# Three edits to the order of work in a four-layer graph kernel: an earlier tile load, fewer tests ahead, logarithms kept together

## The chip, the cores and the metric

The kernel runs on one core of a Trainium2 chip. The time is that of the device, in microseconds (us), for one whole execution. The kernel before has a median of 806.51 us over 3 runs (806.50 to 806.54).

The core has a matmul engine (PE, with its weight loads shown apart as PEld), a vector engine (DVE), a scalar engine that evaluates functions from tables (ACT), a general engine (POOL) and a queue processor (SP). Each runs its own instructions in order. DMA transfers run beside them and are started by SP, ACT or POOL.

## What is computed

`x` is 4096 x 64 and `adj` is a 4096 x 4096 matrix of zeros and ones, about one in 128 a one. Four layers follow each other, each of the form x = x + layer(relu(layernorm(x)), adj):

```python
# layer 0: the entries of a row of adj are weighted by their rank
rank = cumsum(adj != 0, axis=1); deg = rank[:, -1:]
k = minimum(deg, 100);  pos = rank - (deg - k)
w = mask * where(pos > 0, 0.5 ** (k - pos), 0)
out = w @ (h @ weight) + bias
# layer 1: attention over all pairs, then masked by adj
att = adj * sigmoid((2 + 2 * qm @ k.T) / att_scale + att_bias)
support = att @ h1;  out = support / norm(support)
# layer 2: two gated steps
m = adj @ (x @ W); r, z = sigmoid(...); n = tanh(i_n + r * h_n)
x = (1 - z) * n + z * x
# layer 3: hyperbolic aggregation; tanh and artanh of row norms
XW = mobius_matvec(W, X); num = adj @ (gamma * XW); den = adj @ (gamma - 1)
out = expmap0(relu(logmap0(midpoint(num, den, alpha))))
```

Each layer is thus dominated by a product with `adj`. In layer 1 a 4096 x 4096 matrix of sigmoids is also made and masked. In layer 3 artanh is worked out with logarithms.

## The kernel before

**Tiles.** `adj` is used transposed. It is cut into four quarters `q` of 1024 columns and 32 blocks `b` of 128 rows: 128 tiles of 128 x 1024, taken in the order `tiles[n]`, quarter after quarter, with `b` falling from 31 to 0. All tiles stay on the chip as 8-bit floats in `A8` ("A" in the profile). Most come through POOL's queue, whose DMA casts them on the way. The tiles with `direct(n)`, that is n = 0, 1 and every n with n % 8 = 4, come as 32-bit floats through SP's queue into a buffer "whole", and are cast on an engine (`cast0`: tiles 0 and 1 half on ACT and half on DVE, the others on DVE).

**Tests.** The fast path holds only if `adj` is made of zeros and ones. So `checks()` (lines 1102 to 1130) tests every tile in its 32-bit form on DVE, one instruction of 1.22 us each. Tiles that came directly are tested in the buffer that they came in; the other 110 are loaded again through SP, as "whole", for the test alone. The list `depth[0]` says how many such loads may be ahead of the test: 1 at first, 2 from the middle of layer 0's first quarter, still 2 in layer 1, and 4 from layer 2 on. Loads issue as soon as the pool gives a buffer. A last small matmul (flag_ps) collects the result.

**A shared pool.** `b4p` has six buffers of 128 x 1024 floats. They serve the "whole" tiles and the sigmoid tiles "sig" of layer 1 in turn. A new tile waits until the last reader of the buffer's old content is done.

**The planner.** The kernel is built by a Python program that writes every engine's order. `Weave` keeps an estimated time for each engine. The main loops (layer 0's and layer 1's sums, and so on) issue their matmuls directly. Side work is written as generators that yield single operations (`Op`), kept in two lists: `work` for what later stages need, and `back` for the tests. `begin(op)` (line 677) estimates when an operation could start; `fill` issues side operations that fit ahead of the main loop's next one on DVE or ACT with a margin `late`, and `draw` issues what fits beside the matmuls. So a small change of an estimate or of a margin may move many instructions, but only in order.

**Layer 0** (to about 234 us). `stream0` makes running counts with matmuls (cnt, with the constant matrices tri and upd), turns them on ACT or DVE into weights w, and sums w times h (acc, with h in two parts hm and lo). Before that, x is loaded by quarters (`load_x`) and normalized in `pre0`; quarter 3 is needed first. The first loads go through SP in the order tile 0, x of quarter 3, tile 1, x of quarter 2, tile 2 (lines 878 to 883).

**Layer 1** (about 234 to 500 us). For each quarter and each pair of blocks, `stream1` makes the scores on PE (16 matmuls for two half quarters), ACT writes their sigmoid into a "sig" buffer, DVE multiplies it by A, and 16 matmuls add it to acc. The first of two pairs of blocks is weighed at once, the second between older sums (`later`). At the end of each quarter `post1` reads acc out (mt, agg), turns it (ps_n), and prepares layer 2's input (ps_t turns the next one).

**Layer 2** (about 500 to 650 us) runs two steps; each sums A times hm and lo, and works out gates r, z and n (rz and ih on PE, from mx tiles loaded through SP). **Layer 3** (to about 790 us) sums A times S. `pre3` prepares S for each quarter: it forms the norms of h and of the product mxn, calls `lengths` (a maximum and an inverse root on DVE), then `artanh2` (two logarithms on ACT) and a tanh. `post3` does the like for the output. `preload(func)` is a one-element ACT operation that brings in a function's table early; sigmoid and tanh share a table, the logarithm has another.

**Lines in the profile.** All instructions that go through the class `Engine` are recorded with L781; PE's matmuls and transposes have L973 and L977. Which work a row belongs to is told by the tile names.

Of the kernel before, what the change touches and what calls it, by code (L numbers as in the profile page):

```python
# [12 lines left out]
AF = mybir.ActivationFunctionType  # L13
# [580 lines left out]
class Op:  # L594


    def __init__(self, e, dur, ins, outs, run, kinds=()):
        self.e, self.dur, self.ins, self.outs, self.run, self.kinds = e, dur, ins, outs, run, kinds


def names(*aps):
# [3 lines left out]
class Weave:  # L605
# [10 lines left out]
    def __init__(self):  # L616
        self.t = dict.fromkeys("PDAGS", 0.0)
        self.at, self.used = {}, {}
        self.banks = {1: [0.0] * 8}
        self.kind = {}  # L620
        self.work, self.back, self.width = [], [], 2
        self.late = 0.0
        self.quiet = False
        self.dma = 0.0
        self.busy = False
        self.table = None
        self.tiled = 0

    def ready(self, e, ins, outs=(), kinds=()):
        s = 0.0  # L630
# [46 lines left out]
            (self.work if piece in self.work else self.back).remove(piece)  # L677

    def begin(self, op):
        return max(self.t[op.e], self.ready(op.e, op.ins, op.outs, op.kinds))  # L680

    def issue(self, piece):
# [62 lines left out]
TABLES = {AF.Sigmoid: 0, AF.Tanh: 0, AF.Ln: 1, AF.Exp: 2}  # L745


class Engine:
# [12 lines left out]
    def __getattr__(self, name):  # L761
        fn, w = getattr(self.real, name), self.weave

        def call(*args, **kw):
            outs = names(args[0], kw.get("accum_out"))
            ins = names(*args[1:], *(v for k, v in kw.items() if k != "accum_out"))
            n = max(math.prod(a.shape[1:]) for a in args if isinstance(a, bass.AP))
            dur = self.cost(name, n) if name != "dma_start" else 0.1
            if "accum_out" in kw:
                dur += 0.08  # L770

            def run():
                more = 0.0
                if name == "activation" and args[2] in TABLES:
                    more = 1.3 if w.table != TABLES[args[2]] else 0.0
                    w.table = TABLES[args[2]]
                w.book(self.e, dur + more, ins, outs)
                if name == "dma_start":
                    for k in outs:
                        w.land(k, 1.4 if "whole" in k else 0.8)  # L780
                return fn(*args, **kw)  # L781

            if self.later:
                return Op(self.e, dur, ins, outs, run)
            if self.e in "DA":
                w.fill(self.e, w.ready(self.e, ins, outs) + w.late)
            return run()
        return call
# [3 lines left out]
def fast_kernel(ctx: ExitStack, tc: tile.TileContext, t: dict, out: bass.AP, flag: bass.AP):  # L792
# [24 lines left out]
    weave = Weave()  # L817
# [56 lines left out]
    def load_x(q, eng):  # L874
        xq[q] = b2(f"x{q}")
        eng.dma_start(xq[q], x_nm[:, q * QB:(q + 1) * QB, :])

    weave.dma = 0.5
    load0(0)
    load_x(3, Y_)  # L880
    load0(1)
    load_x(2, Y_)
    load0(2)

# [215 lines left out]
    depth = [1]  # L1100
# [246 lines left out]
    def stream1():  # L1347

        acc, behind = [], []

        def add(c, q, i, gs):
            if i == 0:
                acc.append(one(f"acc{c}"))
            for j in range(2):
                b = 2 * i + j
                mm(acc[c][j * D:(j + 1) * D, :], S1[b // QB][:, b % QB, :], gs[c][:, j, :],
                   start=i == 0, stop=i == NB // 2 - 1)

        def add_behind(more=()):
            q, i, gs = behind.pop(0)  # L1360
            for c in (0, 1):
                add(c, q, i, gs)
                if more:
                    more.pop(0)()
                weave.draw(weave.quiet)
            if i == NB // 2 - 1:
                weave.finish()
                weave.add(post1(q, acc[:]))
                acc.clear()

        def turn(q, i, later=None):
            if q == 0 and i % (QB // 2) == 0:
                weave.until((1, i // (QB // 2)), DONE)
            weave.quiet = (1, NQ - 1) not in DONE
            weave.late = 2.0 if weave.quiet else 1.0
            gs = ahead[:] if (q, i) == (0, 0) else []
            for c in range(len(gs), 2):
                ps = score(q, i, c)
                if later is None:
                    gs.append(weigh(q, i, c, ps))  # L1380
                else:
                    later.append(lambda q=q, i=i, c=c, ps=ps: gs.append(weigh(q, i, c, ps)))
                weave.draw(weave.quiet or c == 1)
            behind.append((q, i, gs))
            if i == 8:
                load1(q + 1)

        for q in range(NQ):
            for i in range(0, NB // 2, 2):

                later = []
                turn(q, i)
                turn(q, i + 1, later)
                while len(behind) > 2:
                    add_behind(later)
                for go in later:
                    go()
                if len(behind) > 1:
                    add_behind()
        add_behind()  # L1400
# [193 lines left out]
        yield from pre3(q)  # L1594


    def lengths(s):

        yield DV.tensor_scalar(s, s, NORM_EPS2, None, op0=ALU.max)
        r = yield from rsqrt(s)  # L1600
        n = stat("norm", s.shape[1])
        yield DV.tensor_tensor(n, s, r, ALU.mult)
        return n, r
# [5 lines left out]
    def preload(func):  # L1609

        yield AC.activation(void, tab, func)

    def artanh2(x, between=()):

        nb = x.shape[1]
        xc = stat("axc", nb)
        yield DV.tensor_scalar(xc, x, ARTANH_BOUND, None, op0=ALU.min)
        q, r = stat("at", nb), stat("ln", nb)
        yield AC.activation(q, xc, AF.Ln, bias=ones)
        yield AC.activation(r, xc, AF.Ln, bias=ones, scale=-1.0)  # L1620
        yield from preload(AF.Tanh)
        low = small.tile([P, ST], I32, tag="st", name="flow")[:, :nb]
        yield DV.tensor_scalar(low, xc, 0.25, None, op0=ALU.is_lt)
        x2, p = stat("x2", nb), stat("po", nb)
        yield DV.tensor_tensor(x2, xc, xc, ALU.mult)
        yield DV.tensor_scalar(p, x2, *(2.0 * c for c in ARTANH_POLY[:2]), op0=ALU.mult, op1=ALU.add)
        yield DV.tensor_tensor(p, p, x2, ALU.mult)
        for c in ARTANH_POLY[2:-1]:
            yield DV.scalar_tensor_tensor(p, p, 2.0 * c, x2, op0=ALU.add, op1=ALU.mult)
        yield DV.tensor_tensor(q, q, r, ALU.subtract)  # L1630
        yield DV.scalar_tensor_tensor(p, p, 2.0 * ARTANH_POLY[-1], xc, op0=ALU.add, op1=ALU.mult)
        yield from between
        yield DV.copy_predicated(q, low, p)
        return q
# [3 lines left out]
    def pre3(q):  # L1638
# [9 lines left out]
        for i, v in enumerate((hn, mx)):  # L1648
            sq = b2("sq")
            yield AC.activation(sq, v, AF.Square)  # L1650
            yield DV.tensor_reduce(ss[:, i * QB:(i + 1) * QB], sq, AX.X, ALU.add)
        yield from preload(AF.Ln)
        n, r = yield from lengths(ss)
        mr, c = r[:, QB:], stat("ratio", QB)
        yield DV.tensor_tensor(c, n[:, QB:], r[:, :QB], ALU.mult)
        a = yield from artanh2(n[:, :QB])
# [144 lines left out]
    def post3(parts3, sgn, den, ss):  # L1801

        nb = CB * len(parts3)
        part = [slice(i * CB, (i + 1) * CB) for i in range(len(parts3))]
        vs = [n65[:, :, :D] for u, (n65, al) in parts3]
        yield from head3(len(parts3) - 1, parts3[-1][1], sgn, den, ss)  # L1810
        yield from preload(AF.Ln)
        rd = yield from recip(den)
        n, r = yield from lengths(ss)
        t = stat("t", nb)
        yield DV.tensor_tensor(t, n[:, :nb], rd, ALU.mult)
        ratio = stat("ratio", nb)

        def between():
            yield DV.tensor_tensor(ratio, n[:, nb:], r[:, :nb], ALU.mult)

        a = yield from artanh2(t, between())
        for h, (u, (n65, al)) in zip(part, parts3):
            yield DV.scalar_tensor_tensor(a[:, h], a[:, h], 0.25, al, op0=ALU.mult, op1=ALU.mult)
        yield DV.scalar_tensor_tensor(a, a, ARTANH_MAX, ratio, op0=ALU.min, op1=ALU.mult)
        yield AC.activation(a, a, AF.Tanh)
        yield DV.tensor_tensor(a, a, r[:, nb:], ALU.mult)
        for h, v, (u, (n65, al)) in zip(part, vs, parts3):
            yield DV.scalar_tensor_tensor(v, v, 0.0, rows(a[:, h]), op0=ALU.max, op1=ALU.mult)
            x = X[u // 2][:, (u % 2) * CB:(u % 2 + 1) * CB, :]
            yield DV.tensor_tensor(x, x, v, ALU.add)  # L1830
            yield SY.dma_start(out_nm[:, u * CB:(u + 1) * CB, :], x)
# [8 lines left out]
    weave.add(pre0(NQ - 2))  # L1840
    stream0()
    lead[0] = math.inf
    stream1()
    depth[0] = 4
    for step in range(2):
# [89 lines left out]
```

## Time and profile before

| what | us |
|---|---|
| median of 3 runs | 806.51 |
| the profiled execution, time | 807.01 |
| its span in the trace | 805.1 |
| PE busy | 767.5 |
| DVE busy | 635.6 |
| ACT busy | 432.2 |
| POOL busy | 61.6 |

The profiled execution takes 1.9 us more than its span, and lies 0.5 above the median. The mean granted clock of PE is 0.993. In a row of the profile, "out<-in" names the tile written and the tiles read, x and a number the count of instructions. "[0.81 <-ACT sig]" means that the engine stood idle for 0.81 us before it, and that ACT's work on sig ended that. The groups in which most of the tests and of layer 1 lie are these (busy, mean ns of one | idle before, releaser):

```profile
L781 ACT ACTIVATE sig<-score,fatt_add,fatt_mul 128x512 f32<-128x512 f32 x256 | 179.2, 779 | 57.1 <-DVE whole L781 25.2
L781 DVE TENSOR_TENSOR sig<-sig,A 128x1024 f32<-128x1024 f32 x128 | 154.9, 1223 | 29.9 <-ACT sig L781 25.5
L781 DVE SCALAR_TENSOR_TENSOR whole<-whole 128x1024 f32<-128x1024 f32 x128 | 153.2, 1220 | 4.6 <-DMA whole<-in_adjT 4.0
L973 PE MATMUL score<-qd,kT 64*128 64x512 f32 x512 | 126.3, 612 | 1.5 <-ACT sig L781 1.5
L973 PE MATMUL acc<-sig,S 128*64 128x512 f32 x512 | 120.2, 601 | 4.2 <-DVE sig L781 3.9
```

### The profile page before, as it was taken

To read this page: it belongs to the slowest core of one execution; us is meant where nothing else is said; L and a number is where in the kernel's file an instruction comes from. 1 tells how busy PE (TensorE), PEld (TensorE's weight loads), DVE (VectorE), ACT (ScalarE), POOL (GpSimd) and SP (SyncE) were. 2 spreads that over 40 slices of the span, in tenths; PEclk is the share of its full clock that TensorE was granted. 3 is DMA by queue.
4 is the path that set the end of the run, shared out by engine and by line. 5 is a ranking of instruction groups with operands and counts; after the bars stand their busy time and mean duration, and the time that the engine had idled before them with its cause. 6 is when DMAs were issued, how large, how long until landed. Compare 5 with 4: busy or idle time off the path is not lost.

```text
span 805.1 us, 12309 instructions
## 1 busy us (share of the span) xinstructions
PE 767.5 (95%) x4473; PEld 369.7 (46%) x4494; DVE 635.6 (79%) x1419; ACT 432.2 (54%) x756; POOL 61.6 (8%) x125
## 2 busy tenths in 40 slices
PE   5999999999999999998999999999999999999992
PEld 2334444544443333332333333444444444599992
DVE  6886867777777988988888898978789387685895
ACT  5655555565566777887787785113220245444333
POOL 3333233231000000000000000000000000000000
PEclk9999999999999999999999999999999999999997
DMA  9999999999601033013104006696888300000010
GB/s 220 153 174 193 217 163 207 205 177 207 183 34 40 0 118 93 25 59 99 52 25 130 30 1 210 225 361 215 287 304 313 76 8 20 1 2 2 9 35 17
DMA packets 43956, 98.41 MB, mean 122 GB/s; under 512 B 5104, under 2 KB 20464, under 8 KB 43888
## 3 DMA queue, kind: packets, MB, share of 16 engines
q1 hardware_dynamic: 25888, 78.98, 29.0%
q0 software_dynamic: 15840, 14.42, 19.1%
q10 hardware_dynamic: 2160, 4.14, 1.4%
q8 instruction: 37, 0.61, 0.3%
q14 instruction: 31, 0.25, 0.1%
HBM read 135.54 MB, written 5.24 MB: 175 GB/s over the span
## 4 chain that ended last, share of the span: by engine, by line
PE 80%; DVE 9%; ACT 6%; issue 2%; DMA 1%; SPq 0%; ACTq 0%; DVEq 0%
PE acc L973 50%; PE cnt L973 13%; PE score L973 10%; ACT sig L781 5%; DVE sig L781 3%; DVE whole L781 2%; PE rz L973 2%; PE ps_l L973 2%; DMA whole<-in_adjT 1%; PE ps_t L977 1%; PE ih L973 1%; ACT w L781 1%; DVE ss L781 1%; PE ps_kq L973 1%; DVE w L781 1%
## 5 line engine op out<-in xcount | busy, mean ns | idle before, releaser
L781 ACT ACTIVATE sig<-score,fatt_add,fatt_mul 128x512 f32<-128x512 f32 x256 | 179.2, 779 | 57.1 <-DVE whole L781 25.2
L781 DVE TENSOR_TENSOR sig<-sig,A 128x1024 f32<-128x1024 f32 x128 | 154.9, 1223 | 29.9 <-ACT sig L781 25.5
L781 ACT ACTIVATE w<-cnt 128x512 int16<-128x512 f32 x198 | 111.6, 595 | 88.6 <-PE cnt L973 85.7
L781 DVE SCALAR_TENSOR_TENSOR whole<-whole 128x1024 f32<-128x1024 f32 x128 | 153.2, 1220 | 4.6 <-DMA whole<-in_adjT 4.0
L973 PE MATMUL score<-qd,kT 64*128 64x512 f32 x512 | 126.3, 612 | 1.5 <-ACT sig L781 1.5
L973 PE MATMUL acc<-sig,S 128*64 128x512 f32 x512 | 120.2, 601 | 4.2 <-DVE sig L781 3.9
L973 PE MATMUL acc<-A,hm 128*128 128x512 fp8e4 x512 | 115.4, 379 | 0.0
L973 PEld LDWEIGHTS <-hm 128*128 128x128 bf16 x768 | 73.6, 98 | 90.3 <-issue 8.2
L973 PE MATMUL cnt<-A,ftri 128*128 128x512 fp8e4 x256 | 98.2, 386 | 8.2 <-ACT A L781 8.2
L973 PE MATMUL cnt<-A,fupd 128*128 128x512 fp8e4 x248 | 95.4, 385 | 4.0 <-ACT w L781 1.7
L973 PE MATMUL acc<-S,A 128*128 128x196 bf16 x1024 | 88.0, 246 | 0.0
L973 PEld LDWEIGHTS <-A 128*128 128x128 fp8e4 x1024 | 87.0, 96 | 1.3 <-issue 1.2
L973 PEld LDWEIGHTS score<-qd,kT 64*128 64x128 f32 x512 | 50.5, 186 | 72.0 <-issue 46.7
L973 PE MATMUL acc<-w,hm 128*128 128x512 bf16 x235 | 70.6, 379 | 0.9 <-issue 0.2
L781 DVE TENSOR_SCALAR w<-cnt 128x512 int16<-128x512 f32 x58 | 40.1, 691 | 39.5 <-PE cnt L973 38.3
L973 PEld LDWEIGHTS acc<-sig,S 128*64 128x64 f32 x512 | 32.5, 136 | 83.5 <-issue 40.8
L857 POOL DMA_DIRECT2D A<-in_adjT x110 | 59.9, 546 | 131.5 <-DMA A<-in_adjT 130.7
L973 PEld LDWEIGHTS <-lo 128*64 128x64 bf16 x768 | 39.8, 109 | 50.3 <-issue 21.3
L973 PE MATMUL acc<-A,lo 128*64 128x512 fp8e4 x512 | 58.9, 380 | 0.0
L781 ACT ACTIVATE mt<-acc 64x512 f32<-64x512 f32 x32 | 19.0, 592 | 74.2 <-PE acc L973 64.5
L973 PEld LDWEIGHTS <-ftri 128*128 128x128 bf16 x256 | 24.8, 98 | 47.4 <-issue 20.5
L1676 POOL MEMSET S<- 128x4 bf16 x8 | 0.9, 115 | 537.3 <-DVE xT L781 463.8
(185 smaller groups left out, 634.7 us busy)
## 6 DMA issues: line engine op xcount, KB each, us to landing
whole<-in_adjT SPq DMA_DIRECT2D x128, 512.0 KB, 6.7
A<-in_adjT POOLq DMA_DIRECT2D x110, 128.0 KB, 14.0
qd<-qs SPq DMA_DIRECT2D x16, 128.0 KB, 4.4
mx<-gs SPq DMA_DIRECT2D x16, 128.0 KB, 7.6
xT<-gs SPq DMA_DIRECT2D x8, 256.0 KB, 6.9
x<-in_x SPq DMA_DIRECT2D x6, 256.0 KB, 6.1
xs<-x SPq DMA_DIRECT2D x4, 256.0 KB, 6.0
qs<-qT ACTq DMA_DIRECT2D x4, 256.0 KB, 4.9
```

The costliest lines, as they stand in the source:

```text
L781: return fn(*args, **kw)
L857: nc.gpsimd.dma_start(A8[q][b // 2][:, b % 2, :], a)
L973: nc.tensor.matmul(o, lhsT, rhs, start=start, stop=stop, skip_group_check=True)
L977: nc.tensor.transpose(o, src, ident)
L1676: nc.gpsimd.memset(S3[q, c][:, :, 3 * e:], 1.0)
```

## The change

There are three parts, and no instruction is added or taken away; all of them move work in order.

1. Tile 1 of `adj` is issued on SP's queue ahead of x of quarter 3.
2. Before layer 1 starts, `depth[0]` is set to 1, so only one tile is loaded ahead of its test there; it goes to 4 after layer 1 as before. In the same loop the margin `late` is 0.8 instead of 1.0 once all of layer 1's inputs are made.
3. The preload of the logarithm's table moves from in front of `lengths` to behind its first operation. From there until the second logarithm has been issued, the planner holds back (`held`) every side operation whose function has another table.

```diff
     def begin(self, op):
+        if self.held and op.table not in (None, TABLES[AF.Ln]):
+            return math.inf
         return max(self.t[op.e], self.ready(op.e, op.ins, op.outs, op.kinds))
...
-                return Op(self.e, dur, ins, outs, run)
+                return Op(self.e, dur, ins, outs, run,
+                          table=TABLES.get(args[2]) if name == "activation" else None)
...
     load0(0)
+    load0(1)
     load_x(3, Y_)
-    load0(1)
     load_x(2, Y_)
     load0(2)
...
-            weave.late = 2.0 if weave.quiet else 1.0
+            weave.late = 2.0 if weave.quiet else 0.8
...
-    def lengths(s):
+    def lengths(s, log=False):
 
         yield DV.tensor_scalar(s, s, NORM_EPS2, None, op0=ALU.max)
+        if log:
+            yield from preload(AF.Ln)
+            weave.held += 1
         r = yield from rsqrt(s)
...
         yield AC.activation(r, xc, AF.Ln, bias=ones, scale=-1.0)
+        weave.held -= 1
         yield from preload(AF.Tanh)
...
-        yield from preload(AF.Ln)
-        n, r = yield from lengths(ss)
+        n, r = yield from lengths(ss, True)
...
     lead[0] = math.inf
+    depth[0] = 1
     stream1()
     depth[0] = 4
```

The same replacement of the two lines stands in `pre3` and in `post3`. `Op` takes the new argument `table`, and `Weave` starts with `held` at 0.

More of the change, by code (lines that the diff above doesn't have):

```diff
@@ L594, with __init__ @@
 class Op:
-    def __init__(self, e, dur, ins, outs, run, kinds=()):
+    def __init__(self, e, dur, ins, outs, run, kinds=(), table=None):
         self.e, self.dur, self.ins, self.outs, self.run, self.kinds = e, dur, ins, outs, run, kinds
+        self.table = table
 def names(*aps):
@@ L627, in __init__ @@
         self.tiled = 0
+        self.held = 0
     def ready(self, e, ins, outs=(), kinds=()):
@@ L1810, in post3 @@
         yield from head3(len(parts3) - 1, parts3[-1][1], sgn, den, ss)
-        yield from preload(AF.Ln)
         rd = yield from recip(den)
-        n, r = yield from lengths(ss)
+        n, r = yield from lengths(ss, True)
         t = stat("t", nb)
```

## The prediction

> **What bounds the kernel now.** I read the busy table first, then what the matmul engine (PE) waited for, then PE's stretches by stage, and last the timeline round the waits. The busy table, as engine, busy us, share, instructions:
>
> ```profile
> PE 767.5 (95%) x4473; PEld 369.7 (46%) x4494; DVE 635.6 (79%) x1419; ACT 432.2 (54%) x756; POOL 61.6 (8%) x125
> ```
>
> PE works 767.5 of 805.1 us, so what an edit can bring is what PE loses now: 37.6 us, of which some 14.5 are the tail after PE's last dense work (790.6 to 805.1) and some 21 are single gaps. The waits of PE say who owns them (total us, times, longest):
>
> ```profile
> PE cnt L973 <- ACT A L781: 8.2, 2, 5.9
> PE acc L973 <- DVE sig L781: 3.9, 8, 1.0
> PE ps_n L977 <- ACT sig L781: 2.3, 3, 0.8
> PE ps_o L977 <- DVE xT L781: 1.6, 1, 1.6
> PE score L973 <- ACT sig L781: 1.5, 3, 0.5
> ```
>
> The first row is the start of the kernel, the rows with sig are layer 1, the row with ps_o is layer 3. By stage (length, then busy us of PE, PEld, DVE, ACT, POOL, granted clock, DMA share, GB/s), two quarters of layer 1 and three stretches after it:
>
> ```profile
> 317.11:380.65 63.54, 61.30 (x264) 21.81 (x264) 55.26 (x76) 48.91 (x73) 0.00 (x0) 1.00 0.22 67
> 380.65:444.19 63.54, 61.30 (x264) 21.81 (x264) 55.25 (x76) 48.90 (x73) 0.00 (x0) 1.00 0.22 67
> ...
> 500.00:560.00 60.00, 60.00 (x367) 26.80 (x365) 49.60 (x98) 14.46 (x26) 0.00 (x0) 1.00 0.81 278
> 560.00:650.00 90.00, 90.00 (x543) 38.76 (x543) 67.20 (x118) 17.15 (x30) 0.00 (x0) 1.00 0.69 228
> 650.00:730.00 80.00, 78.37 (x641) 51.72 (x638) 56.88 (x197) 37.72 (x78) 0.81 (x7) 1.00 0.03 8
> ```
>
> Layer 2 leaves PE no gap at all; in layer 1 every quarter repeats the same loss. Inside a quarter the undisturbed cycle is 16 score matmuls (a step of 3.72 us) and 16 acc matmuls (3.58), so 7.30; eight cycles are 58.4, and ps_n and ps_t add about 0.6 each, so about 59.7 against the measured 63.54: near 3.8 us are lost per quarter, all about its boundary. There the timeline (start, us, engine) shows the mechanism:
>
> ```profile
> 378.49 1.23 DVE L781 SCALAR_TENSOR_TENSOR whole<-whole 128x1024 f32<-128x1024 f32 x1
> 379.64 0.08 DVE L781 DVE_READ_ACCUMULATOR whole<-whole 128x1 f32 x1
> 379.64 1.22 DVE L781 TENSOR_TENSOR sig<-sig,A 128x1024 f32<-128x1024 f32 x1
> 379.82 1.45 ACT L781 ACTIVATE sig<-score,fatt_add,fatt_mul 128x512 f32<-128x512 f32 x2 [1.35 <-DVE whole L781]
> 380.65 0.66 PE L977 MATMUL ps_n<-fident,agg 128*128 128x128 f32 x4 [0.81 <-ACT sig L781]
> ```
>
> The sigmoid of ACT writes a buffer of the six-buffer pool that a test (whole) had held. It can't start before the test ends; it stood 1.35 us. PE, which needs ACT to empty the score banks, then stood 0.81. The next score group at 384.82 also takes 4.60 us from start to next start instead of 3.72.
>
> **What the Trainium skill says.** "ScalarE: Activation LUTs", section "What ACT_TABLE_LOAD costs", gives 1283 ns for a table load plus about 1380 ns of drain. This trace agrees with the load (1.28 us) but not with the drain on this path: the load at 708.05 is followed by an ACT instruction at 709.35, 1.30 later. I use 1.28. "TensorE: Matmul & The Clock Gate", Part 1, says that the array runs at half speed until it has been busy for some 3.4 us. The trace agrees in kind: the cnt matmuls step by 0.43 us up to 14.7 us and by 0.215 after. "DMA: Bandwidth & Descriptors", section "Queues, rings and completion order", says that each DMA engine takes the descriptors of a row in ring order. The trace agrees: SP issued tile 0, x, tile 1, and they were usable at 5.23, 5.85 and 9.34.
>
> **The change part by part.**
>
> *Start.* Tile 1 now goes ahead of x (quarter 3). Here is the present wait, and what DVE does meanwhile:
>
> ```profile
> 5.87 0.42 DVE L781 TENSOR_REDUCE mean<-x 128x4 f32<-128x256 f32 x1 [0.19 <-DMA x<-in_x]
> ...
> 9.36 0.63 ACT L781 ACTIVATE A<-whole 128x512 fp8e4<-128x512 f32 x1 [1.72 <-DMA whole<-in_adjT]
> ...
> 10.04 0.58 PE L973 MATMUL cnt<-A,ftri 128*128 128x512 fp8e4 x1 [2.25 <-ACT A L781]
> ```
>
> PE stands 2.25 us for tile 1. The packets of x hold the queue some 1.3 us (x is 256 KB, and tile 1 with 512 KB took the rest of the 3.5 us between landings), so tile 1 should land near 8.0 and PE restart near 8.7: 1.3 gained at most. What pays for it: x lands near 9.3, and its mean, centring and square (0.42+0.42+0.43), which lay in the wait, now come after the cast of tile 1. The normalizing chain on DVE ends about 1.0 later, and the cast of tile 4, now behind hm in DVE's order (14.26 before), starts at about 14.6 and not earlier. Tile 4 is then ready at about 15.3 against 15.00 before. The tiles that POOL's queue brings after it came only 1.1 to 1.3 us ahead of their use, so an earlier PE runs into them. Bounds: 0.3 lost to 1.1 gained. I take 0, because the chain of supply after tile 1 isn't any faster.
>
> *Layer 1.* With two tests ahead, two of the six buffers hold waiting tests and sig turns on four. With one ahead it turns on five. In the order of DVE's instructions after the change, a test stands at least three steps ahead of the sigmoid that takes over its buffer, where it now stands one or two ahead; a step is 1.22 us. So the ACT stalls behind tests (1.35 above, up to 2.3) should go. Per boundary that gives, in PE's own gaps: acc 0.35+0.58, score 0.50, ps_n 0.81, the slow score group 0.88, and 0.17 for each of the four gaps because the ends are modelled (a step is 0.17 longer than the gap alone shows): 3.7 in all. The second and third boundary give 3.7 each. At the first, a test waits for its transfer (DVE idle 1.02 at 292.25), which the change doesn't touch, and about 2.7 goes. The end of layer 1 (two gaps of 0.26, two steps of some 0.17) gives 0.5. Sum 10.6; the bound from below is 0, if the stalls come back one step elsewhere. DVE then works 55.3 less one test of 1.3, so 54.0 of 59.7 us (90%), and ACT 48.9 (82%): tight, but PE stays the slowest. Replaying the orders by hand with these durations left PE about 1.3 us of cover at the tightest sig. I take 10.0. The smaller margin of `late` (0.8 for 1.0) belongs to the same order and isn't priced apart.
>
> *What is moved out of layer 1.* One test fewer per quarter, four or five in all, goes to layer 2: 1.30 us of DVE each beside a PE that is busy anyway (DVE 49.6 of 60 and 67.2 of 90), and one more 512 KB load each in SP's queue, which delivers one per about 1.27 us there. The mx loads of the first gates stand behind one more: 1.3 later against about 1.6 of slack. The second gates' mx loads are issued about five tests later (6 us), but landed some 11 us ahead of use, and their matmuls stand 3 us later in PE's order. Cost 0; without the cover 1.3 to 6.
>
> *Table.* In layer 3 the last gates and the last logarithms share ACT:
>
> ```profile
> 704.29 1.28 ACT L781 ACT_TABLE_LOAD   x1
> ...
> 708.05 1.28 ACT L781 ACT_TABLE_LOAD   x1
> ...
> 709.57 1.28 ACT L781 ACT_TABLE_LOAD   x1
> 710.86 0.69 ACT L781 ACTIVATE z<-rz,gate_b 128x512 f32<-128x512 f32 x1
> ...
> 718.93 0.63 PE L977 MATMUL ps_o<-fident,xT 128*128 128x128 f32 x4 [1.63 <-DVE xT L781]
> ```
>
> The instructions and the number of table loads are the same after the change (64 loads); only their order differs. The squares go first, then the three loads stand in one run, the tanh of the logarithm's chain comes some 3 us earlier, and z and the n gate follow it. The wait of ps_o, 1.63, should be covered, since ps_o also stands four matmul groups later. Bounds: 0 to 1.7 gained; I take 1.6. The tail after 790 keeps ACT's order, and is priced at 0.
>
> *Sum.* −10.0 − 1.6 + 0 = −11.6 on the profiled execution's 807.0, so 795.4. The runs' median (806.51) lies 0.5 below that execution; I keep half of it and say 795.2.
>
> **The rivals.** *Partly (24%).* DVE at 90% is nearly in lockstep with PE, and each boundary still adds two mt and agg steps and one test. If half of the layer-1 loss comes back behind DVE, it is −5.0 − 1.6: 800. For it: the idle time of DVE behind ACT sig is 24.0 us over layer 1, so the two follow one another closely. Against it: that idle time is mostly the same stalls seen from the other side.
>
> *Nothing (4%).* The stalls are only relabelled, since four sig and two tests share six buffers in whatever order. Then only the table's 1.6 and small losses in layer 2 are left: 806.5. Against it: the lead in steps that the new order shows.
>
> *Slower (12%).* With one tile ahead a test finds its data not landed. DVE takes its instructions in order, so every sig behind it stands. The loads need 3.8 to 5.5 us to land in this stage; the new order leaves seven to nine DVE steps (8.5 us and more) between release and test. It decides if that lead shrinks below four steps, as for the test at 292.25, which waited 1.02. At 1.02 for each of some 20 tests, with 0.3 caught by PE's cover, it is +14.4, against −11.6: 809.8.
>
> **How the numbers follow.** The likeliest case, 60%, gives 795.2, with its own range 792.5 to 798. A difference of 0.2% (1.6 us) is about what a measurement of this kernel can tell from no change. The range has to leave out the 12% and the 4% and little else: low end from the full 10.6, the full start gain of 1.1 and 1.7 from the table, 793.4, less 1; high end past the partly case to 804. Faster: 60+24 = 84%; same 4%; slower 12%.
>
> **What would show it.** In the changed profile: "ACT sig <- DVE whole" far below 25.2; quarters of layer 1 near 60 us between ps_n groups; no ps_n, score or acc waits on sig over 0.3 after the first boundary; PE's first wait in tile 1 shorter, but tile 4's matmul still near 15; no wait of ps_o on xT; no PE gap between 500 and 650. A new row "DVE whole <- DMA whole" of several us in layer 1, or a gap at rz or ih in layer 2, would prove me wrong.

## The result and the profile after

The changed kernel takes 797.38 us (median of 4 runs, 797.15 to 798.03) against 806.50 in the same setting: the ratio is 0.9889, 95% interval 0.9872 to 0.9906. It is faster by 9.1 us; 11.3 was forecast. The profiled execution went from 807.01 to 797.43, its span from 805.1 to 795.6.

PE's waits of the changed kernel, as total us, times, longest:

```profile
PE cnt L978 <- ACT A L785: 5.8, 2, 5.4
PE cnt L978 <- DVE A L785: 2.3, 1, 2.3
...
PE acc L978 <- DVE r L785: 1.2, 1, 1.2
PE acc L978 <- DVE sig L785: 1.0, 1, 1.0
```

The waits of ps_n and score on sig are gone, and of eight waits of acc on sig the one at layer 1's very start is left. Two rows are new: one on the cast of tile 4 (DVE A), at the start, and one on DVE r, in layer 3. The two quarters of layer 1 that answer to those shown before (length, then busy us of PE, PEld, DVE, ACT, POOL, clock, DMA share, GB/s) now leave PE no gap, and are 3.4 us shorter each:

```profile
315.77:375.93 60.16, 60.16 (x266) 22.04 (x265) 54.38 (x74) 48.20 (x73) 0.00 (x0) 1.00 0.21 62
375.93:436.08 60.15, 60.15 (x265) 22.04 (x264) 54.38 (x74) 48.14 (x72) 0.00 (x0) 1.00 0.20 62
```

The timeline at the end of the first of them shows why:

```profile
373.77 2.11 ACT L785 ACTIVATE sig<-score,fatt_add,fatt_mul 128x512 f32<-128x512 f32 x3
373.99 1.23 DVE L785 SCALAR_TENSOR_TENSOR whole<-whole 128x1024 f32<-128x1024 f32 x1
...
375.14 2.35 DVE L785 TENSOR_TENSOR sig<-sig,A 128x1024 f32<-128x1024 f32 x2
...
375.93 0.66 PE L982 MATMUL ps_n<-fident,agg 128*128 128x128 f32 x4
```

ACT runs through three sigmoids in a row, past the end of the test, where before it stood 1.35 us for the test's buffer. ps_n starts without a wait. ACT's wait for tests in layer 1 fell from 25.2 us to this (total us, times, longest):

```profile
ACT sig L785 <- DVE whole L785: 1.8, 2, 1.2
```

The same marks in both traces split the difference. The marks are the start of PE's last cnt matmul, the start of the fourth quarter's ps_n, and the end of the last sum of layer 3.

| stretch | before | after | difference | forecast |
|---|---|---|---|---|
| start to the last cnt | 232.23 | 232.64 | +0.41 | 0 |
| to ps_n of the last quarter (layer 1) | 267.50 | 257.38 | -10.12 | -10.0 |
| to the end of the last sum (layers 2 and 3) | 290.89 | 291.15 | +0.26 | -1.6 |
| tail of the span | 14.44 | 14.47 | +0.03 | 0 |

So layer 1 gave what was forecast, and the other two parts gave nothing or cost a little. The experiments ask three things: which edit made layer 1's gain, what moved layer 3, and why an earlier start ends later. All times below are medians of 4 or 5 runs, and each ratio is against the kernel before with its 95% interval. These intervals reach about 1.3 us to either side, so smaller differences between two kernels rest on the marks in their traces, one trace each.

### The profile page after: what moved, and what is told of

Its sections match the earlier page's. It is cut to its first block, busy times and chain, and to the rows that moved or that the text cites. A ratio compares the mean times of both kernels' runs of the same rounds, so it can differ in the third digit from the quotient of the medians.

```text
span 795.6 us, 12294 instructions
## 1 busy us (share of the span) xinstructions
PE 765.4 (96%) x4473; PEld 370.1 (47%) x4494; DVE 636.7 (80%) x1419; ACT 429.9 (54%) x756; POOL 62.1 (8%) x125
## 4 chain that ended last, share of the span: by engine, by line
PE 87%; DVE 6%; ACT 3%; issue 1%; DMA 1%; SPq 0%; ACTq 0%; DVEq 0%
PE acc L978 54%; PE score L978 13%; PE cnt L978 13%; PE rz L978 2%; PE ps_l L978 2%; ACT sig L785 1%; PE ps_t L982 1%; DVE sig L785 1%; DVE ss L785 1%; DMA x<-in_x 1%; PE ih L978 1%; ACT w L785 1%; DVE nt L785 1%; PE ps_kq L978 1%; PE ps_n L982 0%
## 5 line engine op out<-in xcount | busy, mean ns | idle before, releaser
L785 ACT ACTIVATE sig<-score,fatt_add,fatt_mul 128x512 f32<-128x512 f32 x256 | 177.3, 784 | 47.7 <-PE score L978 40.8
L978 PE MATMUL score<-qd,kT 64*128 64x512 f32 x512 | 124.4, 609 | 0.0
L978 PEld LDWEIGHTS <-fupd 128*128 128x128 bf16 x248 | 24.5, 99 | 39.2 <-issue 14.9
```

Source lines behind the costliest of these rows:

```text
L978: nc.tensor.matmul(o, lhsT, rhs, start=start, stop=stop, skip_group_check=True)
```

## Experiments

**Layer 1: fewer tests ahead, or the smaller margin?** One edit alone on the kernel before, in each of two runs:

```diff
 # e3
     lead[0] = math.inf
+    depth[0] = 1
     stream1()
 # e4
-            weave.late = 2.0 if weave.quiet else 1.0
+            weave.late = 2.0 if weave.quiet else 0.8
```

> The kernel before with one edit: one tile ahead of its test in layer 1; the margin stays 1.0. ACT's order is that of before. Theory: the fifth buffer for sig is what frees ACT, so nearly all of layer 1's gain (9 to 10 us) is there and the layer takes the time of the changed kernel; ps_o keeps its 1.63 us wait: about 797 (0.988). Rival: the smaller margin, which moves four of ACT's instructions at each quarter's boundary, does half of it; then this kernel gains 4 to 6 us only (801 to 802).

> The kernel before with the margin 0.8 for 1.0 from layer 1 on, two tiles ahead of the tests. Theory: with four sig buffers the stalls behind the tests stay, so it gains little in layer 1 (0 to 2 us: 804.5 to 806.5) and takes over the layer 3 of the changed kernel (wait of acc on DVE r in place of ps_o on xT, together up to 0.4 slower). Rival: the margin does half of layer 1's gain: 801 to 802.

The depth alone took 796.89 (0.9879, 0.9864 to 0.9894), the margin alone 803.82 (0.9964, 0.9951 to 0.9978). From the last cnt to the last quarter's ps_n, the depth alone needs 257.53 us and the margin alone 264.85, against 267.50 before and 257.38 with both. So 9.97 of the 10.12 us come with the depth. The margin alone is worth 2.65, more than the theory gave it and less than the rival, but it adds only 0.15 to the depth, so what it frees is for the most part what the depth frees too. The one line with the depth does as well as the whole change (796.89 and 797.38). ACT's wait on tests says it too; this is the row for the margin alone, over layer 1, and with the depth alone it is down to 2.0 us in two waits:

```profile
ACT sig L781 <- DVE whole L781: 16.0, 16, 2.1
```

Could it be the tests that leave layer 1, and not the buffers? In the second and third quarter five tests are left where there were six, and that with either edit alone. PE needs 60.14 us for each of these quarters with the depth alone, but 62.35 and 61.77 with the margin alone. So fewer tests don't give the gain by themselves.

**Layer 3: what changed the order there?** The third part was taken out of the changed kernel:

> The changed kernel without the third part: the logarithm's table is preloaded in its old place and nothing is held back. The order of every engine's instructions is the same with and without this part, so the theory is that it does nothing: the time of the changed kernel (0.9889 of before) within 0.1%, with the order table, r, table, logarithms at the last pre3 and the same 1.17 us wait of acc on DVE r. Rival, that of the forecast: the part is what covered the wait of ps_o (1.6 us), so without it the wait is back and the time is 1.2 to 1.6 us longer.

797.36 us (0.9885, 0.9869 to 0.9900), against 797.38 with it. The order of instructions on each engine is the same with and without the part, and PE's marks in layer 3 agree within 0.02 us. The part does nothing in this kernel: it moved no instruction past another on ACT, and `held` held nothing back that changed an order. Yet layer 3's order did change. The margin is set inside layer 1's loop and never set back, so it also steers layers 2 and 3. Here it goes back to its old value:

```diff
     depth[0] = 4
+    weave.late = 1.0
     for step in range(2):
```

> The changed kernel with the margin set back to 1.0 after layer 1. Theory: the margin of 0.8 outlives layer 1 and is what changed the order in layer 3; with 1.0 there the old order is back, with the 1.63 us wait of ps_o and without the 1.17 us wait of acc and the added turns between kinds of matmuls: 0.2 to 0.4 us faster than the changed kernel (797.0 to 797.2). Rival: layer 3's order comes from the tests that moved; then ps_o doesn't wait here either and the time is the same as that of the changed kernel.

The first half of the theory holds: the 1.61 us wait of ps_o on xT is back and that of acc on DVE r is gone, so the order came from the margin. The two runs above agree: with the depth alone ps_o waits 1.6 us, with the margin alone acc waits 1.2 us on DVE r. The time, 797.85 (0.9891, 0.9875 to 0.9908), isn't better, though. The marks tell why, once the start of layer 3's first sum splits the stretch:

| kernel | last ps_n to the first sum of layer 3 (layer 2) | to the end of the last sum (layer 3) | both |
|---|---|---|---|
| before | 195.39 | 95.50 | 290.89 |
| depth alone (e3) | 195.68 | 95.49 | 291.17 |
| margin alone (e4) | 195.28 | 95.12 | 290.40 |
| changed | 196.04 | 95.12 | 291.15 |
| changed, margin reset (e8) | 195.68 | 95.50 | 291.18 |

The new order in layer 3 is worth 0.39, and no more. In layer 2, where PE has no gap, its matmuls stand in another order, and this costs 0.29 with the depth alone and 0.65 with both edits; which turns between kinds of matmuls cost it was not taken apart. So the changed kernel and e8 come out 0.03 apart. Within layer 3 the wait of ps_o is mostly paid back in this way (rows of ACT, DVE and PE from one timeline of the changed kernel):

```profile
694.53 0.69 ACT L785 ACTIVATE r<-rz,gate_b 128x512 f32<-128x512 f32 x1
...
698.18 0.74 DVE L785 SCALAR_TENSOR_TENSOR r<-ih,W,r 128x512 f32<-128x512 f32 x1
...
698.97 7.21 PE L978 MATMUL acc<-S,A 128*128 128x196 bf16 x83 [1.17 <-DVE r L785]
```

The gate r is ready on ACT at 695.22, but DVE takes the product with ih only at 698.18, behind the small operations of the logarithm's chain. The acc matmul reads neither; by elimination it waits for the bank of ih. From start to start of PE's matmuls, ps_o gains 1.8 us and acc loses 1.25, and an added turn between kinds of matmuls takes about 0.2: 0.39 is left.

What ps_o waited for in the old order can be shortened. After the logarithms the preload brings a table for the tanh, and z needs another load right after it. In the next two runs it brings the sigmoid's table instead, which serves the tanh as well. No order changes by this, only table loads fall out (18 for 21):

```diff
-        yield from preload(AF.Tanh)
+        yield from preload(AF.Sigmoid)
```

> The changed kernel with the sigmoid's table preloaded after the logarithms in place of the tanh's, and nothing else; every order is the same but for the table loads. Theory: in the changed order ps_o doesn't wait for z any more and acc waits 1.17 us for DVE's r, which stands behind the logarithms' chain, so one table load fewer in front of z is hidden: 797.4 as the changed kernel. Rival: the load is on the path in this order too, and it is 1 to 2 us faster (795.4 to 796.4).

> Old order of the first loads, one tile ahead, margin 0.8 in layer 1 alone, and after the logarithms the preload brings the sigmoid's table in place of the tanh's (one fewer load on ACT in front of z, since the sigmoid's table also serves the tanh). Theory: start 0.4 better, layer 3 in the old order 0.3 better, and the wait of ps_o falls from 1.63 to about 0.35 because z comes 1.28 us earlier: 797.4 - 0.4 - 0.3 - 1.3 = 795.4. Rival: z isn't what ps_o waits for last, the tanh chain is; then the table load is hidden and the time is 796.7.

On the changed kernel alone it gives nothing: 797.71 (0.9896, 0.9879 to 0.9912). With the old loads and the margin reset it gives 795.28 us (0.9860, 0.9844 to 0.9877), the best of all kernels, 11.4 us below the kernel before, and as its theory had it. Here is ACT in that kernel:

```profile
696.59 1.28 ACT L785 ACT_TABLE_LOAD   x1
697.88 0.20 ACT L785 ACTIVATE void<-tab 128x1 f32<-128x1 f32 x1
697.99 0.67 ACT L785 ACTIVATE z<-rz,gate_b 128x512 f32<-128x512 f32 x1
```

One load, then z at once, where before two loads stood in a row. ps_o isn't among PE's waits any more, and from the last ps_n of layer 1 to the last sum it is 289.37 us instead of the 291.18 of e8. So the wait of ps_o was worth 1.8 us, and the way to it was to take a load away and not to move one.

**The start: why does an earlier second tile end later?** First the loads went back to their old order in the changed kernel:

> The changed kernel with the loads in their old order (x of quarter 3 between tiles 0 and 1). Theory from the trace: the new order costs time, because PE starts its second tile 2.4 us earlier, then stands 2.29 us for tile 4, falls back to half speed and is 0.4 us behind at the end of layer 0. Then this kernel is 0.4 us faster than the changed one: about 0.988 of the kernel before (797.0). Rival: the earlier start is worth its 1 us and is given back elsewhere; then it is 0.5 to 1 us slower than the changed kernel.

796.90 us (0.9883, 0.9868 to 0.9898), 0.5 below the changed kernel, near the 0.4 of the theory. That is too little for the times alone, but the traces agree: in the five kernels with the old order the last cnt starts at 231.65 to 232.23 us, in the nine with the new one at 232.38 to 233.73. The changed start in PE's rows of the timeline:

```profile
7.65 0.58 PE L978 MATMUL cnt<-A,ftri 128*128 128x512 fp8e4 x1 [0.42 <-ACT A L785]
...
12.07 0.38 PE L978 MATMUL cnt<-A,fupd 128*128 128x512 fp8e4 x1
14.73 0.59 PE L978 MATMUL cnt<-A,ftri 128*128 128x512 fp8e4 x1 [2.29 <-DVE A L785]
```

And its stretch from 14 to 20 us (length, busy us of PE, PEld, DVE, ACT, POOL, then the granted clock, DMA share, GB/s):

```profile
14.00:20.00 6.00, 5.27 (x18) 2.06 (x18) 5.45 (x20) 3.15 (x6) 0.69 (x2) 0.72 1.07 264
```

PE takes tile 1 at 7.65 instead of 10.04 and is through with four tiles at 12.1. Tile 4 lands at 13.96, as before (13.86). PE stands 2.29 us, and its clock falls: the duration of a cnt matmul is 0.38 us ahead of the wait and 0.59 after it, and the stretch has a granted clock of 0.72, with 18 matmuls where before there were 25. "TensorE: Matmul & The Clock Gate" (Part 1) of the Trainium skill says that the array returns to half speed after an idle window of about 3.4 us. Here it fell around shorter gaps: in the six kernels with the new order and no filling matmuls, PE idles 1.60 to 2.58 us ahead of tile 4 and its matmuls slow down in each. In the changed kernel that is at once; in the other five, three to six matmuls still take 0.38 us first. So the length of the gap alone doesn't tell when the clock falls. Was it the clock that cost the time? Ten matmuls whose results nobody reads filled the gap:

```diff
+                if c == 0 and n == 4:
+                    ps = one("warm")
+                    for k in range(10):
+                        nc.tensor.matmul(like(ps, a8(q, NB - 1)(0)), upd, a8(q, NB - 1)(0), start=True, stop=True,
...
                 mm(like(cnt[c], a(c)), tri, a(c), start=b == NB - 1, stop=b == 0)
```

> The changed kernel with ten idle matmuls (cast tile 0 times upd, into a spare bank that nothing reads) put in front of the first matmul of tile 4, where PE stands 2.29 us; the order of all else is the same. Theory: the wait lets PE's clock fall, and the seven cnt matmuls after it then step by 0.43 instead of 0.215 us; with PE kept busy they step by 0.215 and PE is 0.6 to 1.0 us earlier by the 40th cnt matmul; at the end 0.5 to 0.9 us faster than the changed kernel (796.5 to 796.9). Rival: the supply of tiles bounds this stretch in any case, or the filling matmuls push the first one of tile 4 back; then the time is that of the changed kernel or 0.5 longer.

```profile
13.13 2.42 PE L1152 MATMUL warm<-A,fupd 128*128 128x512 fp8e4 x10
15.39 0.38 PE L978 MATMUL cnt<-A,ftri 128*128 128x512 fp8e4 x1
```

The clock stays up: tile 4's matmuls take 0.38 us at once, though the first begins at 15.39 for 14.73, as the filling ones end late in this run. The time is 797.53 (0.9894, 0.9877 to 0.9910), as without. In its trace PE is 0.4 us earlier than in the changed kernel at the 41st cnt, and no earlier at the 61st. The rival holds: what the clock gives here is lost again within 20 matmuls. Is the supply of tiles the bound? They do land later in the new order: tiles 7, 8 and 9, which come through POOL's queue, at 19.55, 21.37 and 22.60, before at 18.44, 20.81 and 22.14. One guess was that ACT, running ahead, issues its two loads of x too soon:

```diff
-                    load_x((b - NB + 3) // 2, S_)
...
+                if q == 0 and b in (NB - 3, NB - 5):
+                    k = later_x.pop(0)
+                    nc.scalar.dma_start(xq[k], x_nm[:, k * QB:(k + 1) * QB, :])
```

> The changed kernel with only ACT's two loads of x (quarters 0 and 1) moved two pairs of ACT's evictions further back in ACT's order; the order of all other engines is the same. Theory: with tile 1 early, ACT reaches these loads 2.4 to 2.8 us earlier (9.13 and 12.11 for 11.53 and 14.94), and their 256 KB each take the DMA engines from the tiles that PE needs next, which land 0.5 to 1.1 us later than before. With the loads moved back the tiles from the eighth on land when they did in the kernel before, and the start is 0.4 to 0.7 us better than in the changed kernel: 796.7 to 797.0. Rival: the tiles are late because x of quarter 3 and tile 1 changed places in SP's queue, whatever ACT does; then the landings stay and the time is that of the changed kernel.

The landings came back by half or more (18.86, 21.04 and 22.29), the time didn't: 797.74 (0.9888, 0.9872 to 0.9905). In this trace tile 4 landed at 14.74 and PE was 1.0 behind the changed kernel at the last cnt. So these three landings aren't what costs the time either, or what they gave was lost elsewhere.

The traces show an engine that neither experiment touched: DVE. Here is its wait for x in the changed kernel; then, in the kernel before, in the changed one and in the one with the filling matmuls, the rows where PE waits for the weights w that DVE makes (two w of DVE lie in this stretch; the last row waits for the earlier one):

```profile
8.87 0.42 DVE L785 TENSOR_REDUCE mean<-x 128x4 f32<-128x256 f32 x1 [2.52 <-DMA x<-in_x]
...
32.71 0.69 DVE L781 TENSOR_SCALAR w<-cnt 128x512 int16<-128x512 f32 x1
33.45 0.38 PE L973 MATMUL cnt<-A,fupd 128*128 128x512 fp8e4 x1 [0.26 <-DVE w L781]
...
33.44 0.69 DVE L785 TENSOR_SCALAR w<-cnt 128x512 int16<-128x512 f32 x1
34.18 0.38 PE L978 MATMUL cnt<-A,fupd 128*128 128x512 fp8e4 x1 [0.25 <-DVE w L785]
...
31.08 0.38 PE L978 MATMUL cnt<-A,fupd 128*128 128x512 fp8e4 x1 [0.53 <-DVE w L785]
```

Before, DVE did the first steps on x of quarter 3 while tile 1 was still on its way, and stood 2.35 us between the casts of tiles 0 and 1. Now x lands at 8.85 for 5.85, and DVE stands 0.81 us for tile 1 and 2.52 for x. From there to these w it stands nowhere longer than 0.15 us in either kernel, so it has no slack to make this up: w starts 0.73 later, and so does the 61st cnt matmul, which waits for it. With the filling matmuls PE comes earlier and waits the longer for DVE, 0.53 us at 31.08; so do the two other kernels with these matmuls (0.47 each). So keeping the clock up could bring little. It could bring something where PE is the later of the two: in four of the six traces of the new order without these matmuls, DVE stands 0.17 to 0.32 us for PE at the earlier of these two w. All this is read from traces; no run gives DVE its time back with tile 1 ahead of x.

Three more kernels put the new order of loads into the best one, with the filling matmuls, with the late x, and with both:

> The kernel of e10 with the new order of the first loads and the ten filling matmuls in front of tile 4. Theory: with the clock kept up the new order is worth 0.3 us more than the old one: 795.1. Rival: the filling matmuls don't help, and it is 0.4 us slower than e10.

> The kernel of e10 with tile 1 ahead of x and ACT's two loads of x moved back as in e14. Theory: the start is then no worse than in the old order: 795.0 to 795.3, as e10 or a little better. Rival: the new order of loads costs 0.4 in itself: 795.7.

> The kernel of e15 with the ten filling matmuls in front of tile 4. Theory: supply no longer in the way, PE's clock kept up pays: 0.3 to 0.6 us faster than e15. Rival: the tiles' supply bounds the start in any case, and it equals e15.

They took 796.03 (0.9866, 0.9850 to 0.9882), 795.91 (0.9867, 0.9851 to 0.9884) and 796.22 (0.9875, 0.9859 to 0.9892). None is below 795.28 with the old order, and none bore out its theory. No variant of the new order was seen to pay: it costs about half a microsecond or a little more, and the traces point to x of quarter 3, whose late landing holds up DVE.

## Why the prediction was right, and where it was wrong

**Layer 1** was right in mechanism and size: -10.0 forecast, -10.12 measured. That the size is so close is partly luck, for the shape was off and the misses cancel. The stretch to the first ps_n gained 1.75 (2.7 forecast), the two whole quarters 3.38 and 3.39 (3.7), and the end of the layer 1.60 (0.5). The sum was also added up low: its own terms give 3.8 a boundary and 0.9 at the end, so 11.2 and not 10.6. The margin wasn't priced apart; e4 shows that it could have been (2.65 alone, 0.15 beside the depth).

**Moved tests** cost layer 2 no gap: PE is busy for 90.00 of 90 us from 550 to 640 in the changed kernel. They were priced at 0, though, and the depth alone costs 0.29 there by the changed order of PE. The slower rival (tests that find their data not landed) didn't happen: DVE's wait for a test's transfer in layer 1 stayed at one of 1.0 us. With the depth alone it began to: four such waits, 5.8 us in all, but PE's quarters are no longer than in the changed kernel.

**Table: the step that failed.** The sum had -1.6 for the third part, and the reading of the new order was true: ps_o waits no more. Three things in that step were wrong. The order was given to the third part, which changes no instruction; it came from the margin, which outlives layer 1 (e2, e8). After the wait that went, I didn't look for the next: the product of r with ih had been moved behind the logarithm's chain, and acc stood 1.17 us for it. So layer 3 gained 0.39. And the order of layer 2, which moved as well, was taken to be free and cost 0.65. Measured for all after layer 1: +0.26. (The 64 table loads counted there are 21 in both traces.)

**Start: the term of the sum that was mis-sized.** Taken at 0 within -0.3 to 1.1 gained, it cost 0.41. The argument that supply is no faster was right, since tile 4 landed at 13.96 for 13.86. The restart came at 7.65 and not at the estimated 8.7, because tile 1 landed only 1.24 us after tile 0 (5.91 and 4.67). The estimate had split the 3.5 us between the landings of x and tile 1 by their sizes; the runs show that the third place in SP's queue was slow for either: x, half as large, landed 2.94 us after tile 1. The true cost had been named: the normalizing chain on DVE was to end 1.0 later, and it did (its last step ends at 15.01 for 14.02). But I followed it only to the cast of tile 4, which then came ahead of the chain's end, at 13.98, and not to the w that stand behind it on DVE and that PE waits for. The fall of the clock wasn't foreseen either, but with the clock kept up (e7) the kernel took as long.

The forecast was -11.6 on the profiled execution, which gave -9.58. The difference of 2.0 is these steps: 1.9 from layers 2 and 3, 0.4 from the start, less 0.1 from layer 1 and 0.2 outside these marks.

## What to carry to other kernels

When two kinds of work share a pool of buffers, the number of idle loads in it sets how far the hot loop may run ahead; here one buffer fewer parked in a waiting test gave 10 of 806 us with no instruction added. Before an effect is booked to one part of a diff, compare the program with and without that part: a part may do nothing, and a planner's setting may reach beyond the stage where it is written. Where a wait goes because an order changed, follow the operations that were pushed back, and ask who needs their buffers. Where an earlier start doesn't pay, look for the engine that has no idle time left.

## What the hardware showed that was not expected

The fall of PE's clock around gaps of only 1.60 to 2.58 us, at once or some matmuls later, is one. Another: after the logarithms, a tanh asked for by a one-element preload got a table that doesn't serve the sigmoid that followed (two loads of 1.28 us in a row), while a sigmoid asked for in its place got one that served both. That sigmoid and tanh share a table, as said in the part on the kernel before, holds here only for the table that the sigmoid brings.
